# Fetching the last nine blocks of x2 during the slots' update of the second FFN, into the place of its weights

## The chip, the cores and the metric

The kernel runs on one core of one Trainium2 chip. The metric is the time of one execution on the device, in microseconds (us). Less is better.

## The reference

`x` has the shape [2, 4096, 512] in float32. The reference is a "macaron": a slot FFN at half weight, an attention layer, and the same slot FFN again at half weight, each with a layer norm ahead and a residual addition behind.

```python
x = x + 0.5 * ffn(layernorm(x), ...)     # first FFN
x = x + attn(layernorm(x), ...)          # linear attention with a decaying state
x = x + 0.5 * ffn(layernorm(x), ...)     # second FFN

def ffn(x):                              # 64 slots, D = 512
    S = slot_init * slot_scale, for each batch
    h = gelu([x, mean of S] @ w1.T + b1)
    alpha = softmax of the 8 largest of (h @ w2.T + b2) / (abs(tau) + 0.1), zero elsewhere
    gi = (alpha^T x) / (sum of alpha over the tokens + 1e-8)       # one row per slot
    gx = gi @ gru_wih.T + gru_bih;  gh = S @ gru_whh.T + gru_bhh
    r, z = sigmoid(xr + hr), sigmoid(xz + hz);  n = tanh(xn + r * hn)
    S_new = (1 - z) * n + z * S                                    # the slots' update
    return (alpha @ (S_new @ wv.T + bv)) @ wo.T + bo
```

What matters here is the shape of the FFN: it needs all tokens of a batch to update the slots, and only after the update can it give any token its output. So `x` is read twice by each FFN: once for `alpha` and the slots, once for the residual addition of the output.

## The kernel before

The tokens are cut into 32 blocks of 128 (`NBLK` = 32). A block holds both batches, as a tile of 128 partitions x 2 x 512 float32, 512 KB or 0.524 MB, 4 KB in each partition. The input of the second FFN is called x2. The attention writes it to a DRAM tensor `x2d`.

The second FFN (the phase named "c") has three stages.

1. *Routing and slots* (`ffn_a_phase`, up to the end of `run_merged`). Groups of blocks are normed, routed and summed into the slots in PSUM (`sl`). Blocks 0 to 19 are loaded into a few rotating buffers and lost afterwards; blocks 20 to 31 (`KEEP` = 12) are loaded into tiles of their own (`kx2`) and kept to the end. The routing weights `alpha` of all blocks stay in SBUF (`ak`). During this stage the update's largest weight, `wih`, is loaded into a tile of 24 KB per partition with the tag "big" (`load_wih`, L495).
2. *The slots' update* (`load_rest`, then `gru`). SP issues the loads of the remaining weights (L506), among them `wvt` and `wot` with 8 KB per partition each. `before_c` then issues, also on SP, the fetches of blocks 0 to 10 of x2 (`F3X` = 11 buffers, L616) for the residual addition. TensorE multiplies with `wih` (L529), then with `wv` (L545), then with `wo` (L553). The last step (L555 to L558) splits the result into two parts, `SVh` and `SVl`, of which each has a half for either batch.
3. *The output* (`after_c`). For each block, in order, ScalarE casts its `alpha` (`cast`, L630, four blocks ahead at most), TensorE multiplies it with `SVh` (L488) and `SVl` (L489), VectorE adds the product to the block of x2 in place (L641, two additions a block), and SP issues the store to the output (L642). At the loop's step `t`, from 3 on, ScalarE's queue also issues the fetch of block `t + F3L`, with `F3L` = 8, where that block is one of 11 to 19. These fetches use the eleven buffers again, so each waits until the output that used its buffer has landed. Blocks 20 to 31 need no fetch.

Outside the attention the order on each engine is not written out by hand: the framework orders the traced instructions by priority and by what is ready in its own model, and it inserts the waits. A tile whose tag has one buffer takes the place of the tile that had it before, and its first write waits for the readers of that one. SP's queue, as every queue, issues in order.

Of the kernel before, what the change touches and what calls it, by code (L numbers as in the profile page):

```python
# [9 lines left out]
F32 = mybir.dt.float32  # L10
# [9 lines left out]
P = 128  # L20
D = 512
KC = D // P
# [5 lines left out]
NB = 2  # L28
# [6 lines left out]
HEAD, TAIL = 1, 1  # L35
CFG = {"a": dict(XT=7, XN=2, XH=10), "c": dict(XT=4, XN=2, XH=11)}
KEEP = 12
F3A, F3X, F3L = 4, 11, 8


def win2(ap, n):
# [53 lines left out]
def tile_macaron(  # L95
# [7 lines left out]
    nc = tc.nc  # L103
    V = nc.vector
    T = x.shape[1]
    NBLK = T // P
# [5 lines left out]
    x2d = dr.tile([T, NB, D], F32, tag="x2d", name="x2d")  # L112
# [11 lines left out]
    def flat(a):  # L124
        return a.rearrange("p a b -> p (a b)")
# [180 lines left out]
        V.reciprocal(rs, rs)  # L306
        return mv, rs

    def ffn_a_phase(load, adst, nm, extra, before=None, after=None):

        with tc.tile_pool(name=f"sl{nm}", bufs=1, space=PSUM) as slp, tc.tile_pool(name=f"gp{nm}", bufs=1) as gp:
            sl = slp.tile([P, KC, NB, NS], F32, tag="sl", name=f"sl{nm}")
            wacc = gp.tile([P, GB * NB, NS], F32, tag="wacc", name=f"wacc{nm}")
            gw = {}
            with tc.tile_pool(name=f"f{nm}", bufs=2) as wp, tc.tile_pool(name=f"fs{nm}", bufs=2) as sm, \
                    tc.tile_pool(name=f"ft{nm}", bufs=3, space=PSUM) as ptr, \
                    tc.tile_pool(name=f"fp{nm}", bufs=2, space=PSUM) as ppj, \
                    tc.tile_pool(name=f"fl{nm}", bufs=2, space=PSUM) as ppl:
                groups = split_blocks(NBLK)
                ng = len(groups)  # L320
                pools = (wp, sm, ptr, ppj, ppl)
                st = [dict() for _ in range(ng)]
                items = []
                for g, (b0, n) in enumerate(groups):
                    args = (st[g], nm, g, (b0, n), pools)
                    t0, t1 = b0 / GB, (b0 + n) / GB
                    items += [
                        (t0 - PA["ld"] - n / GB, t1 - PA["ld"] - n / GB, lambda a=args: a_load(*a, load)),
                        (t0 - PA["st"], t0 - PA["st"] + PA["std"], lambda a=args: a_stats(*a)),
                        (t0, t1, lambda a=args: a_norm(*a)),  # L330
                        (t0 + PA["a2"], t1 + PA["a2"], lambda a=args: a_hidden(*a)),
                        (t1 + PA["a2"], t1 + PA["tk"], lambda a=args: a_topk(*a, wacc)),
                        (t1 + PA["tk"], t1 + PA["tk"] + PA["sl"] * n / GB, lambda a=args: a_slots(*a, adst, sl, ng)),
                    ]
                items += extra(gp, ptr, gw, NBLK / GB)
                run_merged(items)
                for i in range(1, GB):
                    nc.gpsimd.tensor_tensor(wacc[:, 0:NB], wacc[:, 0:NB], wacc[:, NB * i:NB * i + NB], ALU.add)
            with ExitStack() as es:
                gr = es.enter_context(tc.tile_pool(name=f"gr{nm}", bufs=1))  # L340
                for _ in load_rest(gr, gw, nm):
                    pass
                if before:
                    before(es)
                gru(gr, sl, wacc[:, 0:NB], gw, nm)
                if after:
                    after()

# [157 lines left out]
            nc.sync.dma_start(gw[n_], src)  # L506
            yield 0.5

    def gru(gp, sl, wacc, gw, nm):

        with tc.tile_pool(name=f"grp{nm}", bufs=1, space=PSUM) as pp:
            wiht, wvt, wot, bot, ghb, hsT, bihn, bvT = (gw[k] for k in "wiht wvt wot bot ghb hsT bihn bvT".split())
            pw = pp.tile([P, NB, NS], F32, tag="po0", name=f"pw{nm}")
            nc.tensor.matmul(flat(pw), ones, flat(wacc), start=True, stop=True)
            rw = gp.tile([P, NB, NS], F32, tag="rw", name=f"rw{nm}")
            V.tensor_scalar(rw, pw, 1e-8 * ASC, XSC, ALU.add, ALU.mult)
            V.reciprocal(rw, rw)
            gi = gp.tile([P, KC, NB * NS], F32, tag="gi", name=f"gi{nm}")
            for k in range(KC):
                V.tensor_tensor(gi[:, k], sl[:, k].rearrange("p b s -> p (b s)"), flat(rw), ALU.mult)  # L520
            v3 = lambda a: a.rearrange("p (b s) -> p b s", b=NB)
            n = gp.tile([P, KC, NB * NS], F32, tag="n", name=f"n{nm}")
            pv = pp.tile([P, KC, NB * NS], F32, tag="pv", name=f"pv{nm}")
            for c in range(KC):
                pg = pp.tile([P, 3, NB * NS], F32, tag=f"pg{c}", name=f"pg{nm}{c}")
                for g in (0, 2, 1):
                    for k in range(KC):
                        f0 = g * D + c * P
                        nc.tensor.matmul(pg[:, g], wiht[:, k, f0:f0 + P], gi[:, k], start=(k == 0), stop=(k == KC - 1),  # L529
                                         skip_group_check=True)  # L530
                rz = gp.tile([P, 2, NB * NS], F32, tag="rz", name=f"rz{nm}{c}", bufs=2)
                h = gp.tile([P, NB * NS], F32, tag="h", name=f"h{nm}{c}", bufs=2)
                for g in range(2):
                    V.tensor_tensor(v3(rz[:, g]), v3(pg[:, g]), bc(ghb[:, 4 * g + c], 1, NB), ALU.add)
                nc.scalar.activation(rz, rz, AF.Sigmoid)
                V.tensor_tensor(v3(h), v3(rz[:, 0]), bc(ghb[:, 8 + c], 1, NB), ALU.mult)
                V.scalar_tensor_tensor(h, pg[:, 2], bihn[:, 8 + c:9 + c], h, ALU.add, ALU.add)
                nc.scalar.activation(h, h, AF.Tanh)

                V.tensor_tensor(v3(n[:, c]), bc(hsT[:, c], 1, NB), v3(h), ALU.subtract)  # L540
                V.tensor_tensor(n[:, c], n[:, c], rz[:, 1], ALU.mult)
                V.tensor_tensor(n[:, c], n[:, c], h, ALU.add)
            for k in range(KC):
                for c in range(KC):
                    nc.tensor.matmul(pv[:, c], wvt[:, k, c * P:(c + 1) * P], n[:, k], start=(k == 0 and c == 0),  # L545
                                     stop=(k == KC - 1), skip_group_check=True)
            sv = gp.tile([P, KC, NB, 2, NS], F32, tag="sv", name=f"sv{nm}")
            for h in range(2):
                V.tensor_tensor(sv[:, :, :, h], pv.rearrange("p k (b s) -> p k b s", b=NB), bc(bc(bvT, 2, NS), 2, NB), ALU.add)
            for b in range(NB):  # L550
                po = pp.tile([P, D], F32, tag=f"po{b}", name=f"gpo{nm}{b}")
                for k in range(KC):
                    nc.tensor.matmul(po, sv[:, k, b].rearrange("p h s -> p (h s)"), wot[:, k], start=(k == 0), stop=(k == KC - 1))  # L553
                ot = gp.tile([P, D], F32, tag=f"ot{b}", name=f"ot{nm}{b}")
                V.tensor_tensor(ot, po, bot, ALU.add)  # L555
                V.tensor_scalar(ot, ot, 0.5 / ASC, None, ALU.mult)
                V.tensor_copy(SVh[:, b], ot)
                V.tensor_tensor(SVl[:, b], ot, SVh[:, b].bitcast(F32), ALU.subtract)  # L558


    def load_x(wp, t):
# [27 lines left out]
    with tc.tile_pool(name="xk", bufs=1) as xk:  # L589
# [17 lines left out]

        f3 = {}
        xo = {}

        def load_out(t, eng):

            xt = keep.get(t)
            if xt is None and t < NBLK:
                xt = f3["pool"].tile([P, NB, D], F32, tag="xt", name=f"cxt{t}", bufs=F3X)
                eng.dma_start(xt, x2d[t * P:(t + 1) * P])  # L616
            xo[t] = xt
# [6 lines left out]
        def after_c():  # L624
            aT = {}

            def cast(t):
                if t < NBLK:
                    aT[t] = f3["pool"].tile([P, NB, P], F32R, tag="aTi", name=f"caT{t}", bufs=F3A)
                    nc.scalar.copy(aT[t], ak[:, t])  # L630

            with tc.tile_pool(name="f3p", bufs=7, space=PSUM) as ppj:
                for t in range(F3A - 1):
                    cast(t)
                for t in range(NBLK):
                    cast(t + F3A - 1)
                    if t + F3L >= F3X:
                        load_out(t + F3L, nc.scalar)
                    for b in range(NB):
                        po = ffn_b(ppj, aT[t], b, f"c{t}")  # L640
                        V.tensor_tensor(xo[t][:, b], po, xo[t][:, b], ALU.add)  # L641
                    nc.sync.dma_start(outr[t * P:(t + 1) * P], xo[t])  # L642

        ffn_a_phase(load_x2, alpha_keep, "c", extra_c, before_c, after_c)


def attention(tc, nc, env):
# [520 lines left out]
```

## Time and profile before

| | us |
|---|---|
| median of 3 runs | 2355.56 |
| lowest and highest of them | 2350.8, 2357.18 |
| the profiled execution | 2342.8 |
| its span, first to last instruction | 2341.0 |

| engine | busy us | share of the span |
|---|---|---|
| TensorE, matmul (PE) | 2100.5 | 90% |
| VectorE (DVE) | 1911.3 | 82% |
| ScalarE (ACT) | 1148.9 | 49% |
| GpSimd (POOL) | 808.5 | 35% |

The mean granted TensorE clock is 0.96 of full speed. The shares are averages over the whole program, most of which is the attention. The second FFN's routing begins near 2005 us, its update runs from about 2250 to 2281 us, and the output takes the rest of the span. Times of a stage are read from the trace, counted from the start of the span. SPq and ACTq are the queues of SP and of ScalarE that issue transfers.

### The profile page before, as it was taken

How to read it: one execution, taken by the hardware profiler on the slowest of the kernel's cores; microseconds unless marked ns; L12 is line 12 of the kernel's file. 1: busy time of each engine (PE TensorE's matmuls, PEld its weight loads, DVE VectorE, ACT ScalarE, POOL GpSimd, SP SyncE). 2: the span in 40 equal slices, each digit the busy share in tenths (PEclk: the TensorE clock that was granted, in tenths of full speed). 3: DMA queues.
4: the chain of work that ended last, by engine and by line, in shares of the span. 5: the costliest groups of instructions: out<-in, count | busy, mean ns of one | idle time of the engine just before them, and what ended most of it. 6: DMA issues, size and time to landing. Idle time of an engine off the chain costs nothing. (4 is left out here: it accounts for less than half of the span.)

```text
span 2341.0 us, 101047 instructions
## 1 busy us (share of the span) xinstructions
PE 2100.5 (90%) x44989; PEld 1585.4 (68%) x44989; DVE 1911.3 (82%) x4876; ACT 1148.9 (49%) x1957; POOL 808.5 (35%) x750
## 2 busy tenths in 40 slices
PE   5878878999999999999999999999999976588886
PEld 5767757767777676777767677777667754377774
DVE  7898538988888888888889888888888886489656
ACT  4677445544445444444545444554444421367631
POOL 2333114433334343333434333444333441134300
PEclk9898989999999999999999999999999988799997
DMA  6332323344443344343334444344444332630049
GB/s 212 123 127 91 96 87 129 119 133 130 142 134 126 123 136 132 128 150 121 126 124 139 128 136 148 120 127 132 135 128 146 102 97 70 219 110 29 2 149 368
DMA packets 176516, 302.75 MB, mean 129 GB/s; under 512 B 27984, under 2 KB 73552, under 8 KB 176080
## 3 DMA queue, kind: packets, MB, share of 16 engines
q1 hardware_dynamic: 161728, 256.45, 32.9%
q10 hardware_dynamic: 14352, 39.85, 5.2%
q8 instruction: 352, 5.77, 1.2%
q14 instruction: 84, 0.69, 0.1%
HBM read 189.23 MB, written 107.00 MB: 127 GB/s over the span
## 5 line engine op out<-in xcount | busy, mean ns | idle before, releaser
L1080 PE MATMUL apo<-wo,Gt 128*128 128x512 f32 x512 | 279.1, 630 | 24.5 <-DVE x1r L1083 24.5
L128 PE MATMUL pv<-xTh,wgh 128*128 128x256 f16 x1024 | 282.1, 275 | 0.0
L129 PE MATMUL pv<-xTh,wgl 128*128 128x256 f16 x1024 | 280.2, 274 | 0.1
L130 PE MATMUL pv<-xTl,wgh 128*128 128x256 f16 x1024 | 280.3, 274 | 0.0
L1014 POOL TENSOR_TENSOR ps<-ST,AC 128x256 f32<-128x256 f32 x128 | 105.5, 824 | 442.4 <-DVE ST L1038 442.4
L128 PE MATMUL pq<-wqh,xTh 128*128 128x384 f16 (+1 forms) x768 | 242.8, 316 | 1.5 <-issue 0.8
L129 PE MATMUL pq<-wqh,xTl 128*128 128x384 f16 (+1 forms) x768 | 240.9, 314 | 0.2 <-DVE xTl L818 0.2
L130 PE MATMUL pq<-wql,xTh 128*128 128x384 f16 (+1 forms) x768 | 240.7, 313 | 0.0
L862 POOL TENSOR_TENSOR qk<-qk,rn 128x512 f32<-128x512 f32 x128 | 137.6, 1075 | 231.7 <-issue 106.7
L836 ACT ACTIVATE qk<-pq,iscA 128x384 f32<-128x384 f32 (+1 forms) x192 | 105.4, 549 | 162.5 <-PE pq L130 139.5
L980 POOL TENSOR_TENSOR KQ<-KQ,Ax 128x512 f32<-128x512 f32 x128 | 168.4, 1315 | 0.4 <-PE pa L959 0.4
L764 DVE TENSOR_TENSOR tmp<-N,MT 128x256 f32<-128x256 f32 (+7 forms) x384 | 161.2, 426 | 5.6
L758 DVE TENSOR_TENSOR tmp<-N,U 128x256 f32<-128x256 f32 (+7 forms) x384 | 164.0, 434 | 1.4
L838 ACT ACTIVATE sq<-pq,iscA 128x384 f32<-128x384 f32 (+1 forms) x192 | 164.7, 858 | 0.0
L1018 PEld LDWEIGHTS pc<-KQ,S 32*32 32x32 f32 x8192 | 123.2, 106 | 50.6 <-ACT Y L1044 31.0
L760 DVE TENSOR_REDUCE MT<-tmp 128x32 f32<-128x256 f32 (+7 forms) x384 | 153.8, 407 | 0.0
L959 PE MATMUL pa<-KQ 32*32 32x64 f32 x8192 | 143.6, 217 | 11.2 <-ACT KQ L872 4.9
L1018 PE MATMUL pc<-KQ,S 32*32 32x64 f32 x8192 | 142.8, 217 | 9.5 <-DVE S L1040 4.9
L959 PEld LDWEIGHTS pa<-KQ 32*32 32x32 f32 x8192 | 121.7, 105 | 37.9 <-issue 14.9
L1035 PEld LDWEIGHTS pc<-X,u 32*32 32x32 f32 x8192 | 120.7, 105 | 38.6 <-issue 21.9
L1035 PE MATMUL pc<-X,u 32*32 32x64 f32 x8192 | 141.9, 216 | 5.2 <-ACT u L1032 3.7
L917 ACT ACTIVATE vg<-pv,iscA 128x512 f32<-128x512 f32 x128 | 88.1, 688 | 96.7 <-PE pv L130 88.7
(304 smaller groups left out, 5760.3 us busy)
## 6 DMA issues: line engine op xcount, KB each, us to landing
d<-a0d ACTq DMA_DIRECT2D x32, 528.0 KB
Ax<-a0d ACTq DMA_DIRECT2D x32, 528.0 KB
xt<-in_x_dram SPq DMA_DIRECT2D x32, 512.0 KB
x<-in_x_dram SPq DMA_DIRECT2D x64, 256.0 KB
x1d<-x SPq DMA_DIRECT2D x64, 256.0 KB
vtd<-vg SPq DMA_DIRECT2D x64, 256.0 KB
kd<-qk SPq DMA_DIRECT2D x64, 256.0 KB
XK<-kd SPq DMA_DIRECT2D x256, 64.0 KB
```

What stands on the lines that cost most here:

```text
L128: nc.tensor.matmul(po, lh, rh, start=start, stop=False, skip_group_check=True)
L129: nc.tensor.matmul(po, ll, rh, start=False, stop=False, skip_group_check=True)
L130: nc.tensor.matmul(po, lh, rl, start=False, stop=stop, skip_group_check=True)
L758: V.tensor_tensor(tv, vw(f, o10 + j0, [[C, n], [0, h], [1, ni]]), vw(U, ou + j0 * 17, [[0, n], [16, h], [1, ni]]), ALU.mult)
L760: yield lambda tv=tv, j0=j0: V.tensor_reduce(vw(mt, n * j0, [[1, n], [n, h]]), tv, AX.X, ALU.add)
L764: V.tensor_tensor(tv, vw(f, o11 + r0 * C, [[C, h], [0, n], [1, nk]]), vw(mt, 0, [[0, h], [n, n], [1, nk]]), ALU.mult)
L838: nc.scalar.activation(sq[:, f0:f1].rearrange("p (q g e) -> p q e g", g=NG, e=C), pq[:, 0:f1 - f0].rearrange("p (q e g) -> p q e g", g=NG, ...
L959: nc.tensor.matmul(pa[s, m], KQ[s, 0, c, b, g], KQ[s, :, c, b, g], start=(m == 0), stop=True, skip_group_check=True, tile_position=(32 * q ...
L980: nc.gpsimd.tensor_tensor(kc, kc, bass.AP(Ax.tensor, Ax[:, :, c].offset, [list(a[0]), [1, 2], list(a[1]), [1, C]]), ALU.mult)
L1018: nc.tensor.matmul(pcv[s, b, g, 0:2 * C], S[s, b, g], KQ[s, :, c, b, g], start=(g == 0), stop=False, skip_group_check=True, tile_position=tp)
L1035: nc.tensor.matmul(pcv[s, b, g, C:3 * C], u[s, b, g], d["X"][s, :, m], start=False, stop=True, skip_group_check=True, tile_position=tp)
L1080: nc.tensor.matmul(po, Gt[:, k, b], wo[:, k], start=(k == 0), stop=(k == KC - 1))
```

## The change

Nine fetches change their place, their queue and their buffers. Blocks 11 to 19 are no longer fetched by ScalarE's queue during the output. `gru` now calls `used` after the products with `wih`, with `wv` and with `wo`. In phase c that is `used_c`. Each call allocates a new tile in the place of the weight just used and has SP fetch blocks into it: six blocks (11 to 16) into the 24 KB of `wih`, two (17, 18) into the 8 KB of `wv`, and one (19) into the place of `wo`. In the output loop `load_out` then only looks the tile up. The eleven buffers of blocks 0 to 10 are not used again.

```diff
-F3A, F3X, F3L = 4, 11, 8
+F3A, F3X = 4, 11
...
-                gru(gr, sl, wacc[:, 0:NB], gw, nm)
+                gru(gr, sl, wacc[:, 0:NB], gw, nm, lambda what: used and used(what, gp, gr))
...
+            used("wih")
             for k in range(KC):
                 for c in range(KC):
                     nc.tensor.matmul(pv[:, c], wvt[:, k, c * P:(c + 1) * P], n[:, k], start=(k == 0 and c == 0),
                                      stop=(k == KC - 1), skip_group_check=True)
+            used("wv")
...
                 V.tensor_tensor(SVl[:, b], ot, SVh[:, b].bitcast(F32), ALU.subtract)
+            used("wo")
...
+        late = {}
+
+        def reuse(t, pool, tag, shape):
+
+            w = pool.tile(shape, F32, tag=tag, name=f"lx_{tag}")
+            f = w.rearrange("p a b -> p (a b)")
+            for i in range(min(shape[1] * shape[2] // (NB * D), NBLK - KEEP - t)):
+                late[t + i] = f[:, i * NB * D:(i + 1) * NB * D].rearrange("p (b d) -> p b d", b=NB)
+                nc.sync.dma_start(late[t + i], x2d[(t + i) * P:(t + i + 1) * P])
+
+        def used_c(what, gp, gr):
+
+            if what == "wih":
+                reuse(F3X, gp, "big", [P, KC, 3 * D])
+            elif what == "wv":
+                reuse(F3X + 6, gr, "wvt", [P, KC, D])
+            else:
+                reuse(F3X + 8, gr, "wot", [P, KC, D])
...
             xt = keep.get(t)
-            if xt is None and t < NBLK:
+            if xt is None and t in late:
+                xt = late[t]
+            elif xt is None and t < NBLK:
                 xt = f3["pool"].tile([P, NB, D], F32, tag="xt", name=f"cxt{t}", bufs=F3X)
                 eng.dma_start(xt, x2d[t * P:(t + 1) * P])
...
-                    if t + F3L >= F3X:
-                        load_out(t + F3L, nc.scalar)
+                    if t >= F3X:
+                        load_out(t, None)
...
-        ffn_a_phase(load_x2, alpha_keep, "c", extra_c, before_c, after_c)
+        ffn_a_phase(load_x2, alpha_keep, "c", extra_c, before_c, after_c, used_c)
```

More of the change, by code (lines that the diff above doesn't have):

```diff
@@ L307, in ln_stats, with ffn_a_phase @@
         return mv, rs
-    def ffn_a_phase(load, adst, nm, extra, before=None, after=None):
+    def ffn_a_phase(load, adst, nm, extra, before=None, after=None, used=None):
         with tc.tile_pool(name=f"sl{nm}", bufs=1, space=PSUM) as slp, tc.tile_pool(name=f"gp{nm}", bufs=1) as gp:
@@ L507, in load_rest, with gru @@
             yield 0.5
-    def gru(gp, sl, wacc, gw, nm):
+    def gru(gp, sl, wacc, gw, nm, used):
         with tc.tile_pool(name=f"grp{nm}", bufs=1, space=PSUM) as pp:
```

## The prediction

> **What bounds the kernel now.** I read the page first, for the stage; then the stage in stretches of time, the queue of SP, the last readers of the weights, and the waits of the output.
>
> The page's slices (58.5 us each) of DMA share and rate, and the chain by line:
>
> ```profile
> DMA  6332323344443344343334444344444332630049
> GB/s 212 123 127 91 96 87 129 119 133 130 142 134 126 123 136 132 128 150 121 126 124 139 128 136 148 120 127 132 135 128 146 102 97 70 219 110 29 2 149 368
> DMA out_dram<-cxt 1%; DVE kx L641 1%; DVE cxt L641 0%; PE pgc L529 0%; PE plc L421 0%; PE gpoc L553 0%; PE fpoc L488 0%; PE fpoc L489 0%; DVE ahlc L457 0%; PE fphc L130 0%; ACT hTc L417 0%; DVE alc L451 0%; PE fphc L129 0%; ACT L442 0%; PE fphc L128 0%
> ```
>
> Only the last slice has the DMA engines at 9 tenths, at 368 GB/s; the slice ahead has 4 tenths. The chain names an output's transfer first, then the additions (L641) that feed the outputs. The change lies wholly in these two slices. Cut finer (columns: stretch, length, busy time per engine, granted clock, DMA share, GB/s):
>
> ```profile
> 2262.00:2274.00 12.00, 9.87 (x73) 8.48 (x72) 6.51 (x23) 1.76 (x5) 0.00 (x0) 1.00 1.03 413
> 2276.20:2284.20 8.00, 7.00 (x24) 4.06 (x23) 6.64 (x13) 1.11 (x3) 0.00 (x0) 1.00 0.01 6
> 2284.20:2290.00 5.80, 5.80 (x25) 3.99 (x23) 5.80 (x11) 1.62 (x4) 0.00 (x0) 1.00 0.99 329
> 2290.00:2312.00 22.00, 12.25 (x28) 7.79 (x28) 11.67 (x19) 3.35 (x9) 0.00 (x0) 0.62 1.04 408
> 2318.00:2324.00 6.00, 6.00 (x25) 3.97 (x24) 6.00 (x11) 2.44 (x6) 0.00 (x0) 1.00 1.05 407
> 2330.00:2338.00 8.00, 0.00 (x0) 0.00 (x0) 1.28 (x3) 0.00 (x0) 0.00 (x0) 0.67 1.04 391
> ```
>
> This is the whole case. From 2284.2 to 2338 the transfers are full: 32 outputs and 9 fetches of 0.524 MB, 16.78 + 4.72 = 21.5 MB. PE and DVE have holes in there (12.25 and 11.67 of 22 us), so the output is bound by transfers. Just ahead, for 8.0 us, the DMA engines move nothing, while the slots' update computes its last products. The queue of SP says why:
>
> ```profile
> 2254.93 13.23 SPq L616 DMA_DIRECT2D cxt<-x2d  x11
> 2283.40 34.23 SPq L642 DMA_DIRECT2D out_dram<-cxt  x20
> 2318.15 15.58 SPq L642 DMA_DIRECT2D out_dram<-kx  x12
> ```
>
> The eleven fetches that have buffers are issued by 2268.2 and landed by 2276.2; SP has nothing more until the first output at 2283.4, whose data start at 2284.2.
>
> **The change part by part.** *Moved: nine fetches, 4.72 MB,* from ACT's queue during the output to SP's during the update. SP sits idle from 2268.2 to 2283.4. Nine issues at the row's pace of 13.23 / 11 = 1.2 us take 10.8 us. What each place must wait for is its last reader (median ns, first and last start):
>
> ```profile
> L529 PE MATMUL pgc<-gic,wihtc x96: 275/275/550, 2252.6 to 2265.7; 128*128 128x128 f32 x96
> L545 PE MATMUL pvc<-nc,wvtc x32: 275/275/377, 2265.8 to 2270.2; 128*128 128x128 f32 x32
> L553 PE MATMUL gpoc<-wotc,svc x16: 592/592/667, 2271.9 to 2278.5; 128*128 128x512 f32 x16
> ```
>
> Blocks 11 to 16 (place of wih) may start at 2266.0, before SP is free for them: no wait. Blocks 17 and 18 (wv) may start at 2270.5, when six more fetches are still queued: no wait. Block 19 (wo) must wait for 2279.1. By then 2276.2 + 8 x 0.524 MB / 413 GB/s = 2286.4 is still covered by the eight before it, so this wait costs nothing either; without that cover it would cost at most 2279.1 - 2276.2 = 2.9 us. Queued behind it on SP are only the outputs, first ready at 2283.4, so 4.3 us of slack.
>
> *What it gains.* The transfers go on through the idle stretch, and the bytes stay the same, so the end comes earlier by what is filled. Lower part: the bare idle time, 8.0 us. Upper part: the slow start of the output (329 instead of 407 GB/s over 5.8 us) is worth 5.8 x 78 / 407 = 1.1 us, if it goes too; 9.1 us together. Against it: outputs alone could run at the slowest row, 391, instead of 407 GB/s: 16.78 MB take 42.9 instead of 41.2 us, so 8.0 - 1.7 = 6.3 us is the lower end. The nearest row of outputs alone (2318 to 2324) has 407, with the full queue that the change will have, so I drop the loss and keep half of the start: **8.6 us**. The other way round: fetches until 2276.2 + 4.72 / 413 GB/s = 2287.6, outputs 41.3 us at 406 GB/s, 2328.9, and 2.8 us from the end of the bulk (2338.2) to the end of the span give 2331.7, 9.3 us less than 2341.0; about 0.3 us comes back in the slower last 8 us.
>
> One rule of the Trainium skill speaks against the change: the page DMA: Bandwidth & Descriptors, section Anatomy of one DMA, gives each transfer a fixed part of about 2.0 us besides bytes / 436e3 (fitted for another issuing path). By that, taken one after another, nine fetches would need 9 x 3.2 = 29 us, an estimate from that page, more than the update leaves. The trace disagrees for queued transfers: eleven issued in 13.23 us at 413 GB/s. What transfers in series would do here is the last rival.
>
> *Removed: nine issues from ACT.* They block its casts, and with them PE and DVE:
>
> ```profile
> 2250.43 1.32 ACT L630 CAST caT<-ak 128x256 fp32r<-128x256 f16 x4 [1.51 <-PE slc L482]
> 2251.77 1.28 ACT L535 ACT_TABLE_LOAD   x1
> 2287.70 8.32 ACTq L616 DMA_DIRECT2D cxt<-x2d  x4
> 2296.12 0.41 ACT L630 CAST caT<-ak 128x256 fp32r<-128x256 f16 x1 [8.54 <-DMA cxt<-x2d]
> ```
>
> ```profile
> PE fpoc L488 <- ACT caT L630: 9.7, 4, 5.2
> ```
>
> ```profile
> DVE cxt L641 <- PE fpoc L489: 10.3, 11, 3.1
> ```
>
> (The last two: us in total, times, longest.) I cost the removal at nothing for the end: DVE's 10.3 us of waiting go, its additions end about 10 us earlier, near 2321, but the outputs behind them still need the DMA engines until about 2329. Late next is therefore the outputs' transfer, as now. Even at DVE's own pace of 14.43 us for 24 additions, 1.20 us a block, it stays ahead of the outputs' 1.29 us (0.524 MB at 407 GB/s). A second buffer round disappears too: no block of 0 to 10 is reused, so no fetch waits for an output to land. PE, DVE and POOL execute the same instructions.
>
> **The sum.** The profiled execution took 2342.8 us (span 2341.0), so it would take 2334.2. The runs shown have a median of 2355.56, 12.8 us more, from 2350.8 to 2357.18; nothing in the trace places that difference in this stage, so I take the 8.6 us off the median: **2347.0**, 0.37% less. A measurement of this kernel can tell about 0.3% from no change, 7.1 us, so faster means below 2348.5.
>
> **The rivals.**
>
> *The bytes leave the output altogether.* If the update hid all nine fetches, 4.72 MB / 407 GB/s = 11.6 us would go: 2344.0. Against it: only 8.0 us ahead of the first output are free, and fetches past 2284.2 push the outputs back. It needs the update's transfers to run faster than the 413 shown, or the start to be slower than I think.
>
> *The fetches start late, so the change does less than it says.* The order on a queue isn't that of the code: above, ACT casts for the output (L630) at 2250.43, ahead of the update's sigmoid (L535). If SP's order or one shared wait held all nine until wo's last reader, at 2279.1, data would start at 2279.9 (0.8 us after issue, as from 2283.4 to 2284.2), 3.7 us of the idle stretch would remain, and the gain would be 4.9 us: 2350.7, within 0.3%. For it: the order isn't visible before. Against it: the loads' readers end 9 and 13 us apart, and the SP row shows the fetches in the order of the code.
>
> *Slower: blocks that share a place wait for each other.* Six blocks now lie in one tile, two in another. If dependencies were kept for the whole tile, the addition into block 12 would wait until block 11's output, which reads the same tile, has landed, and so on: six such waits (12 to 16, and 18). Each then runs in series: two additions 1.2 us, 0.8 us to the first data, 1.29 us of data, and up to 1.5 us to the landing seen (the last data at 2339.5, the end at 2341.0), 4.8 us in place of 1.29: 3.5 us x 6 = 21 us. Less 8.6, that is 12.4 us slower, 2368.0; it decides against the change from 1.4 us a wait. Against it, a tile with two parts in this trace:
>
> ```profile
> 2279.92 0.47 PE L488 MATMUL fpoc<-SVh,caT 128*128 128x512 f32 x1 [0.88 <-DVE otc L555]
> ```
>
> ```profile
> 2280.27 0.43 DVE L557 CAST SVh<-otc 128x512 fp32r<-128x512 f32 x1
> ```
>
> PE reads the first half of SVh at 2279.92 while DVE writes the second half only at 2280.27: parts are told apart. For transfers into a re-used place the trace shows no such case.
>
> *The nine fetches run in series.* From rows: 0.8 us to the first data and 1.27 us of data each, 2.1 us x 9 = 19 us from 2276.2 to 2295.1, outputs 41.3 us behind them and 2.8 us to the end, 2339.2: a gain of 1.8 us, 2353.8. The SP row speaks plainly against it, so it gets little. It is the fixed part of the page DMA: Bandwidth & Descriptors of the Trainium skill.
>
> **How the numbers follow.** Forecast (6.3 to 9.1 us gained): 0.70, of which 0.62 lands beyond 7.1 us and 0.08 within it, by the spread of the runs. All bytes hidden: 0.08, faster. Late start: 0.10, no change that can be told. In series: 0.02, likewise. Waits in a shared tile: 0.08, slower. Something unseen: 0.02, slower. Together 0.70 faster, 0.20 same, 0.10 slower. Range: 2344.0 of the first rival less 2.5 us for the spread of the runs, 2341.5; 2350.7 of the second plus 3.3 us for the spread, 2354.0; the slower rival is left out. The likeliest case alone: 2343.5 to 2351.
>
> **What would show it.** Right: fetches of blocks 11 to 19 on SP from about 2268 to 2280, none on ACT; the stretch 2276 to 2284 at about 410 GB/s; the first outputs' data from about 2287.6; DVE's additions in one run of 39 us, without waits for PE, ended near 2321; the DMA engines full to the end of the span near 2332. Wrong: a hole in the transfers before or after the first output (late start, shared waits), additions L641 that wait for an output to land, or outputs alone below 400 GB/s.

## The result and the profile after

| | median us | lowest to highest | runs |
|---|---|---|---|
| before | 2357.86 | 2346.8 to 2366.66 | 20 |
| after | 2348.75 | 2343.18 to 2353.88 | 20 |

The ratio after / before is 0.9959, with a 95% interval of 0.9946 to 0.9972. On 2357.86 us that is 9.7 us less (6.6 to 12.7). The change makes the kernel faster, by 0.41%. That is more than the 0.3% from which the prediction counts a kernel as faster, though the lower end of the interval, 0.28%, lies just under it. The bound of 2348.5 us that the prediction gives for this is 0.3% below its median of three runs; 0.3% below the 2357.86 us measured here is 2350.8.

The profiled execution of after has a span of 2348.2 us, *longer* than the 2341.0 of before. That is no contradiction. The stage that the change touches can be cut out of either trace: from SP's issue of the first of the update's loads (L506) to the end of the span. It starts at 2250.41 us in the trace before and at 2266.48 in the trace after, and it takes 90.59 and 81.72 us. Ahead of it all five engines have the same instructions in the same order, line numbers aside. The start alone moved by 16.1 us, and it moves as much between all the executions below (2250.0 to 2271.5 us), with the kernel before once more at 2265.95. So the experiments are read by the length of the stage, which varies little: 90.59 and 90.35 us in two profiles of before, 81.72 and 82.26 in two of after. The means differ by 8.5 us. Two profiles of one kernel differ by up to 0.54 us, so smaller differences between single profiles aren't read.

To compare a time of the trace after with one in the prediction, take off 16.07 us. First the queue of SP in the trace after (start, time spent, line, what it issues):

```profile
2271.00 13.15 SPq L639 DMA_DIRECT2D cxt<-x2d  x11
2285.15 6.67 SPq L621 DMA_DIRECT2D lx_big<-x2d  x6
2292.82 1.56 SPq L621 DMA_DIRECT2D lx_wvt<-x2d  x2
2295.39 0.32 SPq L621 DMA_DIRECT2D lx_wot<-x2d  x1
2299.49 11.73 SPq L665 DMA_DIRECT2D out_dram<-cxt  x11
2322.84 16.00 SPq L665 DMA_DIRECT2D out_dram<-kx  x12
```

Nine fetches now stand between the eleven and the first output, which is issued at 33.0 us of the stage, as before. The last fetch goes out just behind the last reader of `wo`, which starts at 2294.5 and takes 0.6 us:

```profile
L555 PE MATMUL gpoc<-wotc,svc x16: 592/592/667, 2288.0 to 2294.5; 128*128 128x512 f32 x16
```

The same stage in stretches (as in the prediction: length, busy time per engine, clock, DMA share, GB/s):

```profile
2292.20:2300.20 8.00, 7.00 (x23) 3.98 (x22) 6.64 (x13) 1.11 (x3) 0.00 (x0) 1.00 1.03 410
2300.20:2304.00 3.80, 3.80 (x18) 3.04 (x17) 3.80 (x7) 1.62 (x4) 0.00 (x0) 1.00 1.02 406
2306.00:2328.00 22.00, 22.00 (x74) 11.01 (x74) 22.00 (x38) 7.47 (x19) 0.00 (x0) 1.00 1.05 406
2340.00:2345.00 5.00, 0.00 (x0) 0.00 (x0) 0.00 (x0) 0.00 (x0) 0.00 (x0) 0.50 1.03 385
```

The first row is the 8.0 us that held 6 GB/s before: now 410. The third has PE and DVE busy through all 22 us, where before they had 12.25 and 11.67. The last row has no engine busy at all, and the transfers still run. The groups of the output in the trace after say the same (busy us, mean ns of one, then the idle time just before them and its releaser):

```profile
L488 PE MATMUL fpoc<-SVh,caT 128*128 128x512 f32 x64 | 28.6, 451 | 1.0 <-DVE otc L557 0.9
L664 DVE TENSOR_TENSOR kx<-fpoc,kx 128x512 f32<-128x512 f32 x24 | 14.4, 681 | 0.0
L664 DVE TENSOR_TENSOR cxt<-fpoc,cxt 128x512 f32<-128x512 f32 x22 | 13.4, 682 | 0.1
L653 ACT CAST caT<-ak 128x256 fp32r<-128x256 f16 x28 | 11.3, 406 | 32.6 <-PE fpoc L489 32.6
```

The additions no longer wait (10.3 us before), PE no longer waits for casts (9.7 us before), and ScalarE waits for PE alone. VectorE ends at 2336.0 us, or 69.5 us of the stage. The span ends 12.2 us later.

### The profile page after: what moved, and what is told of

Read it like the earlier page. It is cut to its first block, busy times and chain, and to the rows that moved or that the text cites. A ratio compares the mean times of both kernels' runs of the same rounds, so it can differ in the third digit from the quotient of the medians.

```text
span 2348.2 us, 101030 instructions
## 1 busy us (share of the span) xinstructions
PE 2102.1 (90%) x44989; PEld 1583.9 (67%) x44989; DVE 1916.8 (82%) x4876; ACT 1148.5 (49%) x1957; POOL 808.2 (34%) x750
## 5 line engine op out<-in xcount | busy, mean ns | idle before, releaser
L1055 ACT COPY u<-pc 128x256 f32<-128x256 f32 x128 | 47.6, 372 | 180.9 <-PE pc L1051 131.9
```

## The experiments

Theory 1 is that of the prediction: the output is bound by the bytes that the transfers move, and the gain is an idle stretch of the transfers that gets filled. Theory 2: the gain comes from the waits of ScalarE, TensorE and VectorE that go. Theory 3: what is fetched ahead of the outputs costs them nothing. Each kernel was profiled once; those with a ratio were also timed in further executions.

| kernel | stage us |
|---|---|
| before, before again | 90.59, 90.35 |
| after, after again | 81.72, 82.26 |
| fetches' code after wo (late_all) | 81.68 |
| fetches wait for wo (late_wait) | 86.44 |
| six of nine early (six_early) | 84.55 |
| before, fetches on GpSimd's queue (pool_queue) | 90.29 |
| after, 16 more VectorE copies (dve_fill) | 81.92 |
| after, 32 more VectorE copies (dve_fill32) | 83.82 |
| after without the nine fetches (no_fetch) | 79.82 |
| after with seven fetches (seven_fetch) | 80.20 |
| after, small loads in the routing (small_early) | 80.92 |
| after, one more block kept (keep13) | 80.64 |

### Do the waits of the engines matter?

First the fetches are taken off ScalarE's queue in the kernel before, and nothing else, so that they no longer hold up its casts:

```diff
-                        load_out(t + F3L, nc.scalar)
+                        load_out(t + F3L, nc.gpsimd)
```

> The kernel before, but the nine fetches during the output are issued by GpSimd's queue, which has nothing else to do there, and no longer stand ahead of ScalarE's casts. Theory 1: the transfers have the same bytes and the same idle stretch, so the stage stays at 90.6 us, within 0.7 us. Theory 2: the casts run ahead and TensorE and VectorE lose their waits, so most of the 8.9 us go: 82 to 84 us.

It took 90.29 us. The waits of VectorE and TensorE in its output:

```profile
DVE cxt L641 <- DMA cxt<-x2d: 8.5, 5, 2.3
DVE cxt L641 <- PE fpoc L489: 2.8, 3, 1.6
```

```profile
PE fpoc L488 <- DVE cxt L641: 7.3, 8, 1.5
```

The casts no longer hold anyone up: PE's 9.7 us of waiting for ScalarE are gone. VectorE now waits 8.5 us for the fetches themselves. The wait changed its name and the end stayed where it was. This kernel doesn't take all waiting away, so the other direction was tried too: work is added to VectorE in the changed kernel.

```diff
                         V.tensor_tensor(xo[t][:, b], po, xo[t][:, b], ALU.add)
+                    if t % 2 == 0:
+                        scr = f3["pool"].tile([P, D], F32, tag="scr", name=f"scr{t}")
+                        V.tensor_copy(scr, xo[t][:, 1])
```

> The changed kernel with one more VectorE copy of 128x512 (0.43 us, into a scratch tile) after the additions of every second block: 16 copies, 6.9 us, spread over the output. Theory 1: VectorE ends its additions about 10 us ahead of the last transfer, so the stage stays at 81.7 us, within 0.7 us. Theory 2: the output's pace is that of the computing engines, so the stage grows by about 6.9 us to 88.6 us.

It took 81.92 us. In the trace of this kernel:

```profile
L664 DVE TENSOR_TENSOR kx<-fpoc,kx x24: 679/679/683, 2329.5 to 2345.3; 128x512 f32<-128x512 f32 x24
L667 DVE COPY scr<-kx x6: 415/415/415, 2331.3 to 2344.9; 128x512 f32<-128x512 f32 x6
```

VectorE ends at 2346.0, which is 74.5 us of this stage, 5.0 us later than in after (the copies overlap a little with their neighbours, so they cost less than 6.9). The end of the stage doesn't move. The same edit without its `if` has twice the copies:

> The changed kernel with a VectorE copy of 128x512 after the additions of every block: 32 copies. Sixteen moved the end of VectorE's additions by 5.0 us, to 74.5 us of the stage, and the stage stayed at 81.9 us. Theory 1: 32 move it to about 80 us, which is past the point where the outputs still have work queued, so VectorE now sets the pace and the stage takes 83 to 84.5 us. Theory 2: 82.0 + 10.5 = 92.5 us.

It took 83.82 us, and VectorE ends with the last of the copies:

```profile
L666 DVE COPY scr<-kx x12: 427/460/468, 2321.7 to 2338.1; 128x512 f32<-128x512 f32 x12
```

That is at 2338.6, or 80.3 us of this stage. The 32 copies, 14 us by their own durations, moved the end of VectorE by 10.8 us, and that cost 1.8 us at the end of the stage. So VectorE's end can move by some 9 us in the changed kernel before VectorE sets the pace. The first of these three runs doesn't decide, as the waiting stayed. The other two leave theory 2 little: a delay of VectorE as large as the 10.3 us of waits that the change took away costs about 2 of the 8.5 us.

### Is it the idle stretch?

The first try only moved the code of all nine fetches behind the product with `wo`:

```diff
-            if what == "wih":
+            if what == "wo":
                 reuse(F3X, gp, "big", [P, KC, 3 * D])
-            elif what == "wv":
                 reuse(F3X + 6, gr, "wvt", [P, KC, D])
-            else:
                 reuse(F3X + 8, gr, "wot", [P, KC, D])
```

> All nine fetches stand behind the last product with wo, in the same places as in the changed kernel. Measure: the stage, from SP's issue of the first of the update's loads (L506) to the end of the span; 90.6 us before, 81.7 us after. Theory 1 (the gain is idle time of the transfers that gets filled): the transfers stop when the eleven fetches have landed and begin again 0.8 us after the product with wo, so 3.7 us stay idle and the stage takes about 85.4 us. Theory 2 (the gain is that ScalarE, TensorE and VectorE no longer wait for fetches during the output): the fetches are off ScalarE's queue here too and all of them land before the output needs them, so the stage takes 81.7 us as after. Theory 3 (fetches ahead of the outputs cost the output nothing): 81.7 us as well.

It took 81.68 us, which agrees with theories 2 and 3 and not with the number given for theory 1. But the edit did not do what it was meant to do. SP issued the six fetches at 2287.81 us, 18.8 us into its stage, and after issues them at 18.7. The framework orders by what is ready, and the place of `wih` is free early wherever the code asks for it. So this run doesn't separate the theories. The next one forces the order on SP's queue:

```diff
...
-            if what == "wih":
-                reuse(F3X, gp, "big", [P, KC, 3 * D])
-            elif what == "wv":
-                reuse(F3X + 6, gr, "wvt", [P, KC, D])
-            else:
-                reuse(F3X + 8, gr, "wot", [P, KC, D])
+            if what == "wo":
+                first = reuse(F3X + 8, gr, "wot", [P, KC, D])
+                with tc.issue_after(first.ins):
+                    reuse(F3X, gp, "big", [P, KC, 3 * D])
+                    reuse(F3X + 6, gr, "wvt", [P, KC, D])
```

> All nine fetches in the same places as in the changed kernel, but on SP's queue block 19 stands first, behind the last product with wo, and the other eight behind it. So none can start before the product with wo has ended. Stage 90.5 us before (90.59, 90.35), 82.0 us after (81.72, 82.26). Theory 1 (the gain is idle time that gets filled): the transfers rest 3.7 us, between the eleven fetches and 0.8 us after the product with wo, so the stage takes 85.4 to 85.7 us. Theory 1 with the slow rate of outputs that follow a rest (374 to 391 GB/s where nothing is fetched, 406 after): if any rest ahead of the outputs brings it, 2.4 us more, 88 us; if only a rest right ahead of them does, 85.5 us. Theory 2 (waits of the output's computing engines): 82.0 us, as all fetches land before they are needed.

It took 86.44 us. Its queue of SP, and its transfers from 26.0 us of the stage on:

```profile
2286.41 0.32 SPq L621 DMA_DIRECT2D lx_wot<-x2d  x1
2286.78 2.96 SPq L621 DMA_DIRECT2D lx_big<-x2d  x6
2289.78 1.13 SPq L621 DMA_DIRECT2D lx_wvt<-x2d  x2
```

```profile
2284.66:2287.40 2.74, 1.86 (x6) 0.59 (x5) 1.61 (x3) 0.00 (x0) 0.00 (x0) 1.00 0.05 13
2287.40:2296.66 9.26, 9.13 (x38) 6.63 (x38) 9.14 (x17) 3.44 (x9) 0.00 (x0) 1.00 1.00 390
2296.66:2300.66 4.00, 4.00 (x15) 2.09 (x14) 4.00 (x8) 1.33 (x4) 0.00 (x0) 1.00 0.99 299
2300.66:2316.66 16.00, 16.00 (x55) 7.87 (x54) 16.00 (x28) 5.31 (x13) 0.00 (x0) 1.00 1.05 406
```

The rest is there, 2.7 us at 13 GB/s. It is 1 us shorter than worked out, as the product with `wo` ended earlier in this run, at 27.8 us of the stage and not at 28.7 as in after. About half of the gain is lost with it: 4.4 us more than after, where 3.4 to 3.7 were expected. The rest is 2.7 us of that. Another part stands in the third row: over 4 us the rate falls to 299 GB/s where fetches give way to outputs, which costs 4 x (406 - 299) / 406 = 1.1 us. The 390 GB/s of the second row, where after has 410, cost another 9.3 x 20 / 410 = 0.5 us. Theory 2 expected 82.0 us here, since all fetches land in time; TensorE and VectorE have no wait in its output. So theory 2 fails here, and theory 1 holds, with a price for the change from fetches to outputs that it didn't name. The run also has all nine fetches on SP's queue, so their leaving ScalarE's queue isn't by itself what gives the gain.

### What do the fetches still cost?

> The changed kernel without the nine fetches: GpSimd fills the nine blocks with zeros instead, so the residual of these blocks is left out of the output. Theory 1: with 4.72 MB less, the first output's data start with its issue, 0.8 us after it, instead of behind the fetches; that is 3.3 us earlier than after, so the stage takes about 78.4 us, or 79.5 us if the slow start of the output (329 instead of 407 GB/s over 5.8 us, 1.1 us) belongs to a start from idle. Theory 3 (the fetches ahead of the outputs cost nothing): 81.7 us as after.

The edit replaces the fetch in `reuse` by `nc.gpsimd.memset(late[t + i], 0.0)`. It took 79.82 us. Taking away 4.72 MB that run in otherwise idle time and a little beyond gains only 2.2 us. That is 0.3 us above the higher of the two numbers of theory 1; theory 3 (81.7) is wrong by 1.9. But the reason given for the higher number, a slow *start*, doesn't hold. The outputs are slow from their start to the end. Stretches 42 to 58 and 70 to 78 us of this stage:

```profile
2299.58:2315.58 16.00, 16.00 (x55) 7.96 (x55) 16.00 (x28) 5.66 (x14) 0.00 (x0) 1.00 1.03 377
2327.58:2335.58 8.00, 0.00 (x0) 0.00 (x0) 0.00 (x0) 0.00 (x0) 0.00 (x0) 0.50 1.03 378
```

Six early fetches, and three left as before:

```diff
-F3A, F3X = 4, 11
+F3A, F3X, F3L = 4, 11, 8
...
-            elif what == "wv":
-                reuse(F3X + 6, gr, "wvt", [P, KC, D])
-            else:
-                reuse(F3X + 8, gr, "wot", [P, KC, D])
...
-                    if t >= F3X:
+                    if F3X <= t < F3X + 6:
                         load_out(t, None)
+                    if t + F3L >= F3X + 6:
+                        load_out(t + F3L, nc.scalar)
```

> Blocks 11 to 16 are fetched early into the place of wih, blocks 17 to 19 by ScalarE's queue during the output, as before the change. Theory 1: six fetches take 7.6 of the 8.0 idle us, so nearly the whole gain is there: stage 82 to 83 us. Theory 2: the gain goes with the fetches taken out of ScalarE's queue, six of nine: 90.6 - 5.9 = 84.7 us.

It took 84.55 us. The number is the one that theory 2 gave, and 1.6 us or more above that of theory 1. The trace says where it comes from (three fetches lie around 2312 to 2316 us, at 320 GB/s):

```profile
2302.00:2312.00 10.00, 10.00 (x39) 6.18 (x38) 10.00 (x18) 3.91 (x10) 0.00 (x0) 1.00 1.00 371
2316.00:2344.00 28.00, 18.39 (x62) 8.95 (x61) 21.79 (x37) 4.87 (x12) 0.00 (x0) 0.88 1.03 385
```

TensorE and VectorE don't wait: PE is busy in all 10 us of the first row, and VectorE has no wait in the whole output. The outputs run at 371 to 385 GB/s and not at 406. At 382 the 16.78 MB take 43.9 us and not 41.3, 2.6 us more, which covers the difference. So theory 1 had the right bound and the wrong rate, and theory 2 met the number without the waits that it rests on.

To see whether a rest ahead of the outputs brings the low rate, seven fetches were kept, just enough that the transfers never rest:

> The changed kernel with seven fetches (blocks 11 to 17); blocks 18 and 19 are filled with zeros by GpSimd, so their residual is left out of the output. Without any of the nine fetches the stage took 79.8 us. Seven fetches take 8.9 us, just more than the 8.0 idle us, so the transfers do not rest. Theory 1 with a slow rate of outputs that follow a rest: outputs at 406 GB/s, stage 82.0 - 2.5 = 79.5 us or a little less, so that moving 3.7 MB more costs nothing. Theory 1 with a slow rate for any output whose queue holds few transfers: 380 GB/s and 81.8 us or more.

It took 80.20 us, between the two numbers. Stretches 26 to 34, 38 to 42 and 42 to 58 us of the stage:

```profile
2276.00:2284.00 8.00, 6.89 (x24) 4.04 (x23) 6.59 (x12) 1.13 (x4) 0.95 (x1) 1.00 1.03 410
2288.00:2292.00 4.00, 4.00 (x15) 1.96 (x14) 4.00 (x8) 1.40 (x4) 0.00 (x0) 1.00 1.05 400
2292.00:2308.00 16.00, 16.00 (x54) 8.04 (x54) 16.00 (x28) 5.47 (x14) 0.00 (x0) 1.00 1.03 383
```

There is no rest, the outputs begin at 400, and after some 4 us they fall to 383. So the rest isn't the cause by itself. 3.67 MB more than in the kernel without fetches cost 0.4 us, which is within what two profiles of one kernel differ by.

### Two versions that should move less at the critical time

One loads `bihn`, `bvT` and the broadcast of `bo` during the routing, through a second load list at 0.8 to 0.9 of it:

```diff
...
-            return [(0.5 * ng, 0.8 * ng, lambda: load_wih(gp, gw, "c"))]
+            return [(0.5 * ng, 0.8 * ng, lambda: load_wih(gp, gw, "c")), (0.8 * ng, 0.9 * ng, lambda: load_small(gp, gw, "c"))]
```

> The changed kernel, and bihn, bvT and the broadcast of bo (0.27 MB, many of them small packets) are loaded during the routing, right after wih, when the transfers have little to do, instead of at the start of the update. Theory 1: the transfers are full from the weights' loads to the end, so time saved at their start comes out at the end, up to the 3.3 us by which the first output waits behind fetches: the stage takes about 79.2 us (78.4 to 80.2), and the kernel some 2.5 us less than after. Theory 2: the output's pace is that of the computing engines, so nothing changes: 81.7 us.

> The changed kernel once more, for its ratio beside the one above on the same chip, and for how far the stage's length varies: every theory expects 81.7 us within 0.5 us, and a ratio to before near 0.996.

The stage took 80.92 us, 1.1 us less than the mean of after, where 2.8 were expected. The ratios to before, on one chip, are 0.9951 (0.9936 to 0.9967) for this version and 0.9935 (0.9919 to 0.995) for after again, so the whole kernel shows no gain. (After again took 82.26 us, 0.1 us outside its expectation.) The other one keeps one block more, at the price of a buffer of the routing:

```diff
-CFG = {"a": dict(XT=7, XN=2, XH=10), "c": dict(XT=4, XN=2, XH=11)}
-KEEP = 12
+CFG = {"a": dict(XT=7, XN=2, XH=10), "c": dict(XT=4, XN=2, XH=10)}
+KEEP = 13
...
-            else:
-                reuse(F3X + 8, gr, "wot", [P, KC, D])
```

> The changed kernel with one block more kept from the routing (KEEP = 13, so eight fetches), paid for with one buffer less of the normed halves in the routing (XH = 10). Theory 1: 0.524 MB less, so the stage takes 82.0 - 1.3 = 80.7 us; the routing ahead of it may lose some of that. Ratio to before about 0.995, or as after where the routing gives it back.

The stage took 80.64 us, as expected, and the ratio is 0.9941 (0.9923 to 0.9959), which can't be told from the two ratios of after, 0.9959 and 0.9935. In both versions part of what was saved came back in the rate of the last outputs. Stretch 58 to 70 us of the stage, small_early, then keep13, where after has 408 GB/s:

```profile
2324.28:2336.28 12.00, 7.02 (x24) 3.34 (x23) 10.42 (x18) 1.16 (x3) 0.00 (x0) 1.00 1.04 393
```

```profile
2313.46:2325.46 12.00, 8.10 (x28) 3.87 (x26) 11.50 (x20) 1.45 (x4) 0.00 (x0) 0.95 1.04 388
```

Neither is shown to beat the changed kernel. The kernel before, profiled once more, gave the noise of the stage (90.35 us) and of its start:

> The kernel before once more, for how far the stage's length and the time ahead of the stage vary: every theory expects a stage of 90.6 us within 0.7 us; the start of the stage, 2250.4 us in the profile before and 2266.5 us in the one after, may lie anywhere between.

## Why the prediction was right

The forecast was 8.6 us off the median and 2347.0 us; measured were 9.7 us by the ratio and 2348.75 us. The stage shows 8.5 us. That 8.5 falls on 8.6 is in part luck, as two profiles of one kernel differ by more than that.

- **The bound.** "The output is bound by transfers" holds. The holes in PE and DVE from which it was read don't show it alone; the runs do: the end of VectorE can move by some 9 us before the stage grows (dve_fill, dve_fill32), and the last 12.2 us of the span have no addition left.
- **What each place waits for.** As worked out. Blocks 11 to 18 were issued without a rest of the transfers, and block 19 at 2295.39, 0.3 us behind the end of its last reader. The outputs behind it had their slack: the first is issued at 33.0 us of the stage in both traces.
- **The gain.** The idle stretch of 8.0 us is filled, at 410 GB/s. Of the two terms beside it, the slow start (1.1 us, of which half was taken) went altogether: 406 GB/s from 2300.2 on. It wasn't a start alone, though. In the trace before, the outputs moved at 359 and 369 GB/s for 4.2 us and at 266 from 2288.4 to 2290.4, where the first of ScalarE's fetches join them; that last stretch is more than half of the 1.1 us. The slower outputs were dropped for the rate of 407, and in after that was right up to the last 8 us, 385 to 387. So the terms were right for this kernel. For other kernels they would not have been: with six early fetches the gain is 5.9 us, below the lower end of 6.3, with outputs at 371 to 385.
- **The fixed part of a transfer.** By the page DMA: Bandwidth & Descriptors of the Trainium skill, section Anatomy of one DMA, a transfer costs about 2.0 us besides its bytes; the fit is for transfers that GpSimd issues. The nine fetches ran at 410 GB/s through the stretch that used to be idle, so queued behind one another they show no such part.
- **The issues taken from ScalarE**, costed at nothing: right. The waits vanished, and VectorE ended 11 us earlier in the stage than in the trace before (9 us earlier than in before again), with its additions in one run of 39 us as forecast. That none of it reached the end is what dve_fill shows, up to the 2 us that dve_fill32 leaves open.
- **The rivals.** All bytes hidden: no, since without the fetches the stage is 2.2 us shorter. Late start: SP didn't hold the fetches back; where they were made to wait (late_wait), the loss was 4.4 us for 3.7 forecast, of which the rest itself was 2.7. Waits in a shared tile: none, the twelve additions into the place of `wih` ran in one stretch of 7.26 us. In series: no, by the same 410 GB/s.

## What to carry to other kernels

Where a stage is bound by transfers, look just ahead of it for time in which they rest, and count the gain by that time (here 8.0 us of rest and 8.5 us of gain) and not by the bytes moved or by the waits that the transfers cause on the engines. The place of a weight whose last reader has run is a buffer that costs no further memory; in this framework it is free when its reader is done, wherever the code asks for it. And when a gain is smaller than the drift of the rest of the program (here some 20 us), compare the stage and not the span.

## What the runs showed that was not expected

The rate of the outputs isn't one number. The same 32 outputs, from the same queue and issued by the same instructions, ran at these rates in GB/s:

| kernel (early fetches) | 42 to 58 us of the stage | 58 to 70 us | 70 to 78 us |
|---|---|---|---|
| after (9) | 405 | 408 | 387 |
| late_wait (9) | 406 | 406 | 387 |
| dve_fill (9) | 406 | 407 | 387 |
| small_early (9) | 405 | 393 | 366 |
| keep13 (8) | 406 | 388 | 380 |
| seven_fetch (7) | 383 | 381 | 380 |
| six_early (6) | 372 | 382 | 379 |
| no_fetch (0) | 377 | 381 | 378 |

The 366 of small_early contains the end of its transfers; up to 76.7 us of its stage the rate is 386. The 372 of six_early holds its three fetches, at 320. With fewer fetches ahead of the outputs they mostly fell to 380 sooner, but small_early, with nine, falls ahead of after. It isn't the rest alone (seven_fetch has none and falls, late_wait has one and doesn't), nor VectorE's pace (dve_fill). Nor is it how many outputs are queued: by an estimate from the issue times and the bytes moved, dve_fill32 had two to three of them queued from 40 to 56 us of its stage and ran at 401 to 408 GB/s, while no_fetch had two to four and ran at 373 to 379. In the kernel before, with fetches between the outputs, the transfers stayed at 409 up to 70 us. What sets the rate stays open. By these rates, the 16.78 MB of the outputs take 44.4 us at the 378 of no_fetch and 41.3 at 406, up to 3 us more. So taking bytes away gained less than the bytes would at 406.
